# A graph layer's edge loop: six of every thirteen blocks of edges summed by matmuls instead of four of nine, with another beat of the accumulation stages

## The chip, the core and the metric

The kernel runs on one core of a Trainium2 chip. The core's engines work side by side: TensorE (PE in the profile, its weight loads PEld), VectorE (DVE), ScalarE (ACT) and GpSimd (POOL); SyncE (SP) issues most DMA transfers and POOL issues the scatters. Each engine runs its own instructions strictly in order, and semaphores tie them together. The metric is the time of one execution on the device in microseconds (us). Before the change the median of three runs is 2077.85 us (2071.54 to 2080.63).

## What is computed

One layer of a graph network over 6250 nodes with 128 features and 200,000 edges. An edge has a source (`src`), a destination (`dst`, sorted), 20 attributes and a weight. Node features go through a layer norm, a ReLU and a matrix; edge attributes go through a small network that gives a filter; each edge multiplies the gathered row of its `dst` by its filter, and the products are summed by `src`. Cut to what matters:

```python
idx_i, idx_j = src, dst
x = relu(layernorm(x0)) @ W_in
W_ij = shifted_softplus(f_ij @ W_f1 + b_f1) @ W_f2 + b_f2
W_ij = W_ij * f_ij_cutoff
x_ij = x[idx_j] * W_ij
out = segment_sum(x_ij, idx_i, num_segments=6250)
return x0 + shifted_softplus(out @ W_o1 + b_o1) @ W_o2 + b_o2
```

The sources are in random order, so the sum by source is the hard part, and the change is about how it is shared out.

## The kernel before

Edges are worked in quads of 512 (four chunks of 128 edges): 391 quads, and one iteration of a loop written out by hand for each, plus some at the end. In iteration i the kernel does the first matmul of quad i + 1 (`s1_pe`, tile z, L313), the activation of quad i on ACT (`s1_exp`, `s1_ln`, L318 and L323), and for quad i - 1 the gather by a one-hot matmul (`s2_pe_x`, xg, L497), the second matmul (`s2_pe_w`, W, L505), the scaling on ACT (`s2_copy`, xc, L510) and the product on DVE (`s2_m`, L520).

The products are then summed by source in one of three ways, fixed for each quad:

- **Plain quads.** A one-hot comparison on DVE and four fp32 matmuls (`s3_pe`, pp, L532) merge equal sources within a chunk, ACT copies the result (L540), and four indirect DMAs on POOL's queue add the rows to one of four accumulators in HBM (`scatter`, L582, index tile ji).
- **Listed quads.** The product goes straight into four scatters (index tile lji). Rows whose source occurs twice in a chunk go to a list area behind the accumulator instead. Sixteen quads share a window; its list (128 rows per accumulator) is prepared by small steps (`l_eq`, `l_count`, `l_scan`, `l_index`, `l_place`, ...), and twelve iterations after the window's last quad it is read back (`l_load`), summed (`l_sum`), copied by ACT into a tile os (`l_copy`, L475) and scattered once.
- **Grouped quads.** No scatter for the rows themselves. Ranks are worked out for eight grouped quads at a time (`rank_*`). DVE builds one-hots (`perm_oh`, pm, L662) and splits the product into three bf16 parts (`part_rem`, L676); TensorE permutes the 512 rows into 16 groups of 32 slots by source range, in four slices of 128 slots (`permute`, pq, L687, 16 matmuls), and ACT copies the slices out (`perm_out`, tile mst, L693). Rows that found no slot go to an overflow (`over_pe`, po, L702 to L704; `over_out`, mo, L710); two quads' overflow is summed (`over_row`, `over_eq`, `over_sum`), copied by ACT into a tile os (`over_copy`, L746) and scattered once (index tile oji).

Eight grouped quads make a round, and a round has four units, one for each slice s. A unit is 96 small bf16 matmuls (`unit_pe`, un, L781) into four PSUM banks; before it DVE builds eight one-hots (`unit_oh`, so, L766) in the two iterations ahead, and after it DVE adds the four banks to accT in SBUF (`unit_evac`, L792).

PSUM has eight banks: four with the tag A (z, xg, W) and four with the tag B, which permute, overflow, pp, units, lists, ranks, the preparation of nodes (`prep_*`, one group every nine iterations until iteration 216) and others share in the order of the program. A unit takes all four B banks. Tiles rotate through a fixed number of buffers: pm and pt have two, the scattered tiles s four, os two (shared by overflow and lists).

The order is written by hand. `at(i, point, fn, ...)` hangs a step into iteration i at a named point: "L" (loads), "D0" and "D1" (DVE, early), "A0" and "A1" (ACT, before the scaling), "DM" (before the product), "PE2" (TensorE, last in the iteration), "A2", "D2" and "S" (scatters). `clear(i, units)` moves a step out of iterations that hold a unit.

Which quads are grouped follows from `MP0` (the first) and `MPGAPS` (the steps between them, repeated); which iterations hold units from `UOFF`, offsets within one repeat of `MPGAPS` counted from `MP0`; the first that comes five iterations after a round's last quad starts its units. With `MP0 = 8`, `MPGAPS = (2, 2, 2, 3)` and `UOFF = (2, 6)`, quads 8, 10, 12, 14, 17, ... 383 are grouped (168 of them, 21 rounds), and units stand in iterations 28, 32, 37, 41, 46, ... 383, then 389, 391, 393, 395. Of the other 223 quads, 192 in the middle are listed (12 windows) and 31 plain (12 at the start, 19 at the end).

A grouped quad q is permuted two slices in iteration q + 3 and two in q + 4 ("PE2"), with the copies at "A0" of the iterations after. When q + 4 holds a unit (40 quads), all four slices, their copies and the overflow are put into iteration q + 3 instead, ahead of the unit.

After the loop the accumulators are read back, summed with accT, and go through the last two matrices.

Of the kernel before, what the change touches and what calls it, by code (L numbers as in the profile page):

```python
# [7 lines left out]
F32 = mybir.dt.float32  # L8
# [12 lines left out]
P = 128  # L21
# [3 lines left out]
CAP = 32  # L25
OVC = 64
SLOTS = GRP * CAP + OVC
MP0 = 8
MPGAPS = (2, 2, 2, 3)
MPEND = 0  # L30
RND = 8
EXTRA = 0
RKQ = 8
UOFF = (2, 6)
SW = 16
LEARLY = 8
LLATE = 16
# [17 lines left out]
def tile_gnn(ctx: ExitStack, tc: tile.TileContext, x, fB, cT, srcT, srcr, dstr, win_, wf1, wf2, bias, bo1c, wo1,  # L55
             wo2, consts, ident, cmap, out, n_edges):
    nc = tc.nc
# [20 lines left out]
    ZL = 3  # L78
# [4 lines left out]
    units = unit_its(mpq)  # L83
# [11 lines left out]
    LR = P * NW  # L95
# [13 lines left out]
    sp_ = edge.enter_context(tc.tile_pool(name="sp", bufs=4))  # L109
# [31 lines left out]
    zero = accT[:, :ACC_R // ZR]  # L141
# [27 lines left out]

    def zero_list(k, j):  # L170
        v = accs[k][ACC_R:].rearrange("(p t) f -> p (t f)", p=P)
        w = LR // ZL
        nc.sync.dma_start(v[:, j * w:(j + 1) * w], zero[:, :w])

    def xt_load(g):
        o, T = groups[g]
# [294 lines left out]
        mp["L", j]["sum"] = t  # L471

    def l_copy(j):
        s = sp_.tile([P, 132], F32, tag="os", name="os", bufs=2)
        nc.scalar.copy(s[:, :P + 1], mp["L", j].pop("sum")[:, :P + 1])  # L475
        mp["L", j]["os"] = s

# [264 lines left out]
        mp[q]["sum"] = t  # L742

    def over_copy(q):
        s = sp_.tile([P, 132], F32, tag="os", name="os", bufs=2)
        nc.scalar.copy(s[:, :P + 4], mp[q].pop("sum")[:, :P + 4])  # L746
        mp[q]["os"] = s

# [87 lines left out]
    with tc.manual_schedule():  # L836
# [112 lines left out]
        def at(i, point, fn, *a):  # L949
            hooks.setdefault((i, point), []).append((fn, a))  # L950
# [6 lines left out]
        if CE < EP // P:  # L957
            w = (CE + 4 * NS) // 2
# [128 lines left out]
        if spread:  # L1087
            k = clear(mid + 9, busy, 2)
# [3 lines left out]
            k = clear(NQ - 1, busy, 2)  # L1092
# [21 lines left out]
        for r in range(-(-len(mpq) // RKQ)):  # L1114
            i = mpq[RKQ * r]
            at(i - 5, "D2", rank_group, r)
            k = clear(i - 4, units)
            at(k, "PE2", rank_count, r)
            at(k + 1, "D0", rank_own, r)
            k = clear(k + 1, units)  # L1120
# [5 lines left out]
        for w in range((LE - LB) // SW):  # L1126
# [25 lines left out]
            k = clear(i + 1, units)  # L1152
            at(k - 1, "L", l_load, w)
            at(k, "PE2", l_sum, w)
            at(k + 1, "A0", l_copy, w)
            at(k + 1, "DM", l_ji, w)
            at(k + 1, "A2", over_int, ("L", w))
            at(k + 2, "S", over_scatter, ("L", w))
        if LE:
            for k in range(NACC):  # L1160
                for j in range(ZL):
                    at((0, 3, 6, 9)[k] + j + 1, "L", zero_list, k, j)
        for q in mpq:
            at(q + 1, "D2", perm_oh, q)
            at(q + 2, "D2", part_rem, q, 1)
            at(q + 2, "D2", part_rem, q, 2)
            at(q + 2, "A2", part_ext, q)
            if q + 4 in units:
                for s in range(4):
                    at(q + 3, "PE2", permute, q, s)  # L1170
                for s in range(4):
                    at(q + 3, "PE2", perm_out, q, s)
                at(q + 3, "PE2", over_pe, q)
                at(q + 3, "PE2", over_out, q)
            else:
                for s in range(4):
                    at(q + 3 + s // 2, "PE2", permute, q, s)
                    at(q + 4 + s // 2, "A0", perm_out, q, s)
                at(q + 4, "PE2", over_pe, q)
                at(q + 5, "A0", over_out, q)  # L1180
            if q == mpq[-1] and mpi[q] % 2 == 0:
                at(q + 4, "D2", over_none, q)
            if mpi[q] % 2 or q == mpq[-1]:
                at(q + 5, "DM", over_idx, q)
                at(q + 6, "A0", over_dg, q)
                k = clear(q + 6, units)
                at(k, "PE2", over_row, q)
                at(k + 1, "D0", over_eq, q)
                k = clear(q + 8, units)
                at(k, "PE2", over_sum, q)  # L1190
                at(k + 1, "A0", over_copy, q)
                at(k + 1, "DM", over_ji, q)
                at(k + 1, "A2", over_int, q)
                at(k + 2, "S", over_scatter, q)
# [85 lines left out]
    with tc.For_i(0, trips, 1) as ci:  # L1280
# [43 lines left out]
        a = wk.tile([P, P], F32, tag="a", name="fa")  # L1324
# [11 lines left out]
        s = wk.tile([P, P], F32, bufs=1, tag="dg", name="fs")  # L1336
# [112 lines left out]
def sorted_quads(nq):  # L1449
    qs, q = [], MP0  # L1450
    while q < nq - MPEND:
        qs.append(q)
        q += MPGAPS[(len(qs) - 1) % len(MPGAPS)]
    return qs if len(qs) % RND <= EXTRA else qs[:len(qs) // RND * RND]
# [7 lines left out]
def unit_slots(qs, r):  # L1462
    if r == len(qs) // RND - 1:
        return [qs[-1] + 6 + 2 * s for s in range(4)]
    per, end = sum(MPGAPS), qs[RND * r + RND - 1] + 5
    return [i for i in range(end, end + 4 * per) if (i - MP0) % per in UOFF][:4]

# [7 lines left out]
def unit_its(qs):  # L1475
    return {i for r in range(len(qs) // RND) for i in unit_slots(qs, r)}


def clear(i, busy, n=1):
    while any(i + k in busy for k in range(n)):  # L1480
        i += 1
    return i
# [113 lines left out]
```

## Time and profile before

| | |
|---|---|
| Median of three runs | 2077.85 us |
| The profiled execution | 2069.4 us |
| Its span on the core | 2067.6 us |
| Mean granted TensorE clock | 0.963 |
| First scatter issued at | 55.24 us |
| Last scatter issued at, and its duration | 2006.32 us, 1.54 us |
| Scatters (L582): listed, plain, os | 768, 123, 96 |

The profile is of one execution. Its page gives busy time by engine, the span in slices, the DMA queues, a chain of work that ended last and the costliest groups of instructions; the trace behind it can be asked for stretches of time, for waits and for single instructions. In a group's line stand the line, the engine, the operation, the tiles (written from read), the shapes and the count; then busy time in us and the mean duration of one in ns; then the idle time just before these instructions and what ended it. A matmul's duration in the profile reaches into the next one's, since they are pipelined: what one costs is read from the distance between starts. In a timeline line stand the start, the duration (from the first start to the last end of a run of like instructions) and, in brackets, the idle time before it.

### The profile page before, as it was taken

Reading aid. Unit: us, or ns where it says so; the run is one execution under the profiler, and the core shown is the slowest. Engines: PE = TensorE matmul, PEld = TensorE weight load, DVE = VectorE, ACT = ScalarE, POOL = GpSimd, SP = SyncE. Lnnn points to the kernel's source line nnn. Section 1 sums busy time; section 2 is a strip of 40 time slices with the busy share of each in tenths; the row PEclk is TensorE's granted clock in tenths of the full one; section 3 lists DMA queues with packets and bytes.
Section 4 is the critical chain, followed back from the end, with each engine's and each line's share of the span. In section 5 each row is a group of like instructions: output and inputs, shape, how many; then the busy total and the mean of one; then the engine's idle time right before and its main releaser. Section 6 shows DMA issues by size and latency. Waiting matters only on the chain. (4 is left out here: it accounts for less than half of the span.)

```text
span 2067.6 us, 57535 instructions
## 1 busy us (share of the span) xinstructions
PE 1854.7 (90%) x20381; PEld 1285.7 (62%) x20381; DVE 1657.1 (80%) x4448; ACT 1490.1 (72%) x4083; POOL 1631.5 (79%) x1040
## 2 busy tenths in 40 slices
PE   3489997999999999999999999999999999999956
PEld 2356664666666666666666666666666666677734
DVE  3578896898987888988988978979889787787735
ACT  3368775777776788777778777777778678888714
POOL 3578888888877788887878878888888888888774
PEclk9689998999999999999999999999999999999978
DMA  7887766767766776766667666676676676667648
GB/s 240 227 211 150 125 124 109 128 112 135 130 124 106 126 133 117 136 124 122 121 133 123 122 123 117 118 129 107 129 128 116 112 126 111 110 120 131 129 46 242
DMA packets 381187, 272.56 MB, mean 132 GB/s; under 512 B 97727, under 2 KB 341354, under 8 KB 380898
## 3 DMA queue, kind: packets, MB, share of 16 engines
q0 software_dynamic: 143728, 71.30, 34.9%
q1 hardware_dynamic: 236882, 197.50, 33.8%
q8 instruction: 161, 2.64, 0.5%
q14 instruction: 128, 1.05, 0.2%
q10 hardware_dynamic: 288, 0.07, 0.0%
HBM read 154.45 MB, written 114.24 MB: 130 GB/s over the span
## 5 line engine op out<-in xcount | busy, mean ns | idle before, releaser
L582 POOL DMA_INDIRECT acc<-s,lji x768 | 1237.3, 1611 | 266.9 <-issue 184.6
L687 PE MATMUL pq<-pt,pm 128*128 128x387 bf16 x2688 | 527.9, 339 | 27.0 <-DVE pt L676 10.7
L510 ACT ACTIVATE xc<-xg,cb 128x128 f32<-128x128 f32 x1564 | 446.4, 371 | 121.0 <-PE xg L497 113.8
L505 PE MATMUL W<-w,a 128*128 128x128 f32 x3128 | 464.1, 293 | 0.0
L505 PEld LDWEIGHTS W<-w,a 128*128 128x128 f32 x3128 | 388.7, 196 | 42.0 <-issue 2.6
L781 PE MATMUL un<-so,mst 32*128 32x392 bf16 x8064 | 378.3, 331 | 31.9 <-ACT os L746 19.3
L693 ACT CAST mst<-pq 128x387 bf16<-128x387 f32 x672 | 303.1, 481 | 132.6 <-PE pq L687 130.0
L687 PEld LDWEIGHTS <-pm 128*128 128x128 bf16 x2688 | 259.4, 99 | 211.4 <-issue 16.7
L781 PEld LDWEIGHTS <-mst 32*128 32x128 bf16 x8064 | 228.4, 94 | 175.0 <-issue 70.0
L323 ACT ACTIVATE a<-a,con 128x512 f32<-128x512 f32 x391 | 282.3, 722 | 12.7
L582 POOL DMA_INDIRECT acc<-s,ji x123 | 197.0, 1602 | 82.8 <-issue 25.9
L318 ACT ACTIVATE a<-z 128x512 f32<-128x512 f32 x391 | 237.4, 607 | 33.2 <-PE z L313 17.4
L676 DVE TENSOR_TENSOR pt<-pt 128x512 f32<-128x512 f32 x336 | 231.8, 690 | 5.8
L662 DVE TENSOR_SCALAR pm<-iot,pos 128x576 bf16<-128x576 f16 x672 | 221.4, 390 | 0.0
L520 DVE TENSOR_TENSOR s<-W,xc 128x512 f32<-128x512 f32 x192 | 131.9, 687 | 92.9 <-ACT xc L510 86.0
L792 DVE TENSOR_TENSOR accT<-un,accT 128x392 f32<-128x392 f32 x320 | 158.5, 558 | 58.4 <-PE un L781 58.2
L766 DVE TENSOR_SCALAR so<-iot,mst 128x392 bf16<-128x392 f16 x672 | 191.2, 344 | 5.5 <-PE un L781 5.4
L582 POOL DMA_INDIRECT acc<-os,oji x96 | 155.6, 1621 | 31.1 <-issue 16.2
L497 PE MATMUL xg<-wn,oh 63*128 63x128 bf16 x1564 | 157.2, 222 | 14.5 <-ACT xc L510 8.1
L313 PE MATMUL z<-ft,ws 123*128 123x512 bf16 x391 | 151.6, 388 | 16.1 <-POOL b2rep L927 9.3
L494 PE MATMUL W<-b2rep,onesb 64*128 64x512 bf16 x391 | 153.8, 393 | 0.0
L520 DVE TENSOR_TENSOR pt<-W,xc 128x512 f32<-128x512 f32 x168 | 115.2, 686 | 34.9 <-ACT xc L510 29.4
(209 smaller groups left out, 2431.1 us busy)
## 6 DMA issues: line engine op xcount, KB each, us to landing
rb<-reld SPq DMA_DIRECT2D x391, 64.0 KB
fsd<-f SPq DMA_DIRECT2D x49, 480.0 KB
ft<-fsd SPq DMA_DIRECT2D x195, 120.0 KB
sb<-src SPq DMA_DIRECT2D x169, 128.0 KB
fb<-in_fB_dram SPq DMA_DIRECT2D x49, 320.0 KB
ft<-fsd SPq DMA_DIRECT2D x195, 80.0 KB
wn<-tab SPq DMA_DIRECT2D x782, 15.8 KB
acc<-s,lji POOLq DMA_INDIRECT x768
```

Source lines behind the costliest of these rows:

```text
L318: nc.scalar.activation(a, st[q]["z"], AF.Exp)
L323: nc.scalar.activation(a, a, AF.Ln, bias=half, scale=0.5)
L505: nc.tensor.matmul(W[:, c, :], st[q]["a"][:, c * P:(c + 1) * P], w2, start=False, stop=(c == 3))
L510: nc.scalar.mul(xc[:, c, :], st[q]["xg"][:, c, :], late["c", q // CQ][:, 4 * (q % CQ) + c:4 * (q % CQ) + c + 1])
L520: nc.vector.tensor_tensor(m[:, :, :P], st[q]["W"], st[q]["xc"], op=ALU.mult)
L582: nc.gpsimd.indirect_dma_start(out=accs[k][:rows, :], out_offset=bass.IndirectOffsetOnAxis(ap=ji, axis=0), in_=s, in_offset=None, compute_ ...
L662: nc.vector.tensor_scalar(pm[:, c], iot[:, :SLOTS], rk[r]["pos"][:, 4 * j + c:4 * j + c + 1], None, op0=ALU.is_equal)
L676: nc.vector.tensor_tensor(pt[:, :, k * P:(k + 1) * P], a, high(a), op=ALU.subtract)
L687: nc.tensor.matmul(t[:, :PW], mp[q]["pm"][:, c, s * P:(s + 1) * P], high(mp[q]["pt"][:, c:c + 1, :PW])[:, 0], start=(c == 0), stop=(c == 3))
L693: nc.scalar.copy(mp[q]["ms", s][:, :PW], mp[q].pop(("q", s))[:, :PW])
L766: nc.vector.tensor_scalar(so, iotw[:, :GN], w[:, 3 * P // 2:3 * P // 2 + 1], None, op0=ALU.is_equal)
L781: nc.tensor.matmul(ts[g][:, :GN], mp[q]["ms", s][v, k * P:(k + 1) * P], mp[q]["oh"][v], start=(q == qs[0] and k == 0), stop=(q == qs[-1] a ...
```

## The change

`MP0` becomes 5, `MPGAPS` (2, 2, 2, 2, 2, 3) and `UOFF` (2, 7, 11). So six of 13 quads are grouped, from quad 5 on: 5, 7, 9, 11, 13, 15, 18, ... 384, 176 of them in 22 rounds. Three iterations of 13 hold a unit: 25, 29, 33, 38, 42, 46, 51, ... 384, then 390, 392, 394, 396. Of the other 215 quads 176 are listed (11 windows) and 39 plain (20 at the start, 19 at the end).

With these places, no grouped quad has a unit in iteration q + 4, and 56 have one in q + 3. The diff widens the rule for putting all four slices together: if q + 3 or q + 4 holds a unit, all four slices, copies and overflow go into the other one of the two.

The tile os gets four buffers for two. With 11 windows an accumulator's list area has 1408 rows, which three pieces do not divide evenly by columns, so the zeroing computes each piece's bounds. The rank steps for the first eight grouped quads move from iteration 3 to iteration 0, and with them everything that hangs on the first quads' places.

```diff
-MP0 = 8
-MPGAPS = (2, 2, 2, 3)
+MP0 = 5
+MPGAPS = (2, 2, 2, 2, 2, 3)
...
-UOFF = (2, 6)
+UOFF = (2, 7, 11)
...
     def zero_list(k, j):
         v = accs[k][ACC_R:].rearrange("(p t) f -> p (t f)", p=P)
-        w = LR // ZL
-        nc.sync.dma_start(v[:, j * w:(j + 1) * w], zero[:, :w])
+        a, b = j * LR // ZL, (j + 1) * LR // ZL
+        nc.sync.dma_start(v[:, a:b], zero[:, :b - a])
...
     def l_copy(j):
-        s = sp_.tile([P, 132], F32, tag="os", name="os", bufs=2)
+        s = sp_.tile([P, 132], F32, tag="os", name="os", bufs=4)
...
     def over_copy(q):
-        s = sp_.tile([P, 132], F32, tag="os", name="os", bufs=2)
+        s = sp_.tile([P, 132], F32, tag="os", name="os", bufs=4)
...
-            if q + 4 in units:
+            if q + 3 in units or q + 4 in units:
+                k = q + 3 if q + 4 in units else q + 4
                 for s in range(4):
-                    at(q + 3, "PE2", permute, q, s)
+                    at(k, "PE2", permute, q, s)
                 for s in range(4):
-                    at(q + 3, "PE2", perm_out, q, s)
-                at(q + 3, "PE2", over_pe, q)
-                at(q + 3, "PE2", over_out, q)
+                    at(k, "PE2", perm_out, q, s)
+                at(k, "PE2", over_pe, q)
+                at(k, "PE2", over_out, q)
             else:
```

## The prediction

> **What bounds the kernel now.** I read the page's totals first, then the costliest groups, the busy time by window, the waits, and last the timeline of single stretches. The totals put two engines near the span:
>
> ```profile
> PE 1854.7 (90%) x20381; PEld 1285.7 (62%) x20381; DVE 1657.1 (80%) x4448; ACT 1490.1 (72%) x4083; POOL 1631.5 (79%) x1040
> ```
>
> POOL's 79% hides more, as the groups show (busy and mean ns, then idle before and its cause):
>
> ```profile
> L582 POOL DMA_INDIRECT acc<-s,lji x768 | 1237.3, 1611 | 266.9 <-issue 184.6 <-DVE s L520 25.0 <-DMA acc<-s,lji 22.0
> L687 PE MATMUL pq<-pt,pm 128*128 128x387 bf16 x2688 | 527.9, 339 | 27.0 <-DVE pt L676 10.7 <-DVE rt L651 6.3 <-ACT mst L693 3.6
> L781 PE MATMUL un<-so,mst 32*128 32x392 bf16 x8064 | 378.3, 331 | 31.9 <-ACT os L746 19.3 <-DVE pr L627 6.8 <-ACT s L540 2.4
> ```
>
> A scatter takes 1.61 us, and the timeline of POOL has 0.30 us before nearly each one that waits for nothing: 1.91 us of queue. There are 768 + 123 + 96 = 987 (lists, plain quads, sums): 1885 us, between the first at 55 us and the end of the last at 2007.9. So POOL really waits only some 68 us in those 1953. By windows (busy of PE, PEld, DVE, ACT, POOL, then clock, DMA share, GB/s):
>
> ```profile
> 300.00:400.00 100.00, 84.58 (x942) 57.97 (x941) 74.90 (x201) 68.26 (x189) 81.63 (x51) 0.91 0.64 115
> 900.00:1000.00 100.00, 91.15 (x1012) 63.58 (x1011) 85.22 (x233) 74.93 (x210) 79.64 (x50) 0.98 0.70 125
> 1700.00:1800.00 100.00, 98.86 (x1119) 67.60 (x1119) 79.72 (x207) 79.79 (x219) 83.85 (x53) 1.00 0.65 109
> 1950.00:2000.00 50.00, 39.87 (x536) 29.16 (x534) 29.48 (x86) 15.83 (x50) 39.96 (x26) 0.93 0.47 56
> ```
>
> TensorE is 91 to 99% busy through the loop. POOL does 50 to 53 scatters per 100 us, and 52.4 would fill it: it has slack in the middle, none late. After 1950 POOL drains a backlog while the others fall idle. From a list quad's product (DVE L520) to its first scatter it is 20 us around 200 to 300 us, 0.3 to 8 in the middle and 8 to 10 between 1530 and 1780 (those rows compared). The four s buffers allow four list quads, some 35 us at this pace, so after 300 us POOL holds nobody through them. It does through the ring of two os tiles, once for long:
>
> ```profile
> ACT os L746 <- DMA acc<-os,oji: 18.2, 2, 13.8
> ```
> ```profile
> 361.25 0.27 ACT L746 COPY os<-osum 128x132 f32<-128x132 f32 x1 [13.77 <-DMA acc<-os,oji]
> ```
> ```profile
> 361.56 2.80 PE L781 MATMUL un<-so,mst 32*128 32x392 bf16 x32 [14.18 <-ACT os L746]
> ```
>
> Copies at 322.8 and 337.7 (the second a list's sum) had filled both; POOL reached the first one's scatter only at 357.9, behind lists, and the next copy and TensorE's unit stood until then. So: TensorE with ACT and DVE sets the pace in the middle, POOL early, in the tail, and nearly so from 1300 us.
>
> **What the parts cost.** TensorE's prices, from starts in the timeline:
>
> ```profile
> 1904.62 1.56 PE L687 MATMUL pq<-pt,pm 128*128 128x387 bf16 x8
> 1906.11 0.25 PE L702 MATMUL po<-pt,pm 128*64 128x131 bf16 x1
> ...
> 1906.94 0.39 PE L494 MATMUL W<-b2rep,onesb 64*128 64x512 bf16 x1
> ...
> 1908.26 0.38 PE L313 MATMUL z<-ft,ws 123*128 123x512 bf16 x1
> 1908.58 4.16 PE L781 MATMUL un<-so,mst 32*128 32x392 bf16 x96
> 1912.67 0.39 PE L494 MATMUL W<-b2rep,onesb 64*128 64x512 bf16 x1
> ```
>
> A grouped quad: two permute halves of 1.49, the overflow 0.83, four eighths of a unit of 4.09 (2.05), half of orow and osum (0.22 each: 0.22), ranks (27.2 us of rkp and rko over 168: 0.16). Sum 6.24. A listed quad: lcnt, lsum, orow, lid, lpre, 56.8 us over 192: 0.30. A plain quad: pp, 0.89 by its spacing. Every quad has 1.54 of W, xg and z besides.
>
> *More grouped quads.* 168 become 176, listed 192 become 176, plain 31 become 39. TensorE: +8 x 6.24 - 16 x 0.30 + 8 x 0.89 = +52 us. POOL: 768 to 704, 123 to 155, sums 96 to 99: 958 scatters, -29 x 1.91 = -55 us. DVE, by the same division of rows (L662, L676, L766, L792 and the small ones: 5.8 a grouped quad, 1.0 a listed, 1.0 a plain): +38. ACT (L693 1.80, others 1.1 a grouped quad; 0.06 a listed; 1.0 a plain): +30. Per iteration TensorE's bare work goes from 1.54 + (4 x 6.24 + 5 x 0.30)/9 = 4.48 to 1.54 + (6 x 6.24 + 7 x 0.30)/13 = 4.58 us, POOL's from 22.3 x 1.91/9 = 4.73 to 31.4 x 1.91/13 = 4.62. The bounds swap nearly. DVE's and ACT's added work lies beside TensorE's.
>
> *Places of the units.* Before, 40 quads do all their permuting right before a unit, so all four B banks wait for ACT's copies when the unit begins: those units take 4.38 instead of 4.09. After, 56 quads do it in the iteration after a unit, whose banks DVE empties in four adds of 0.56 (2.2 us), while W, xg and z take 1.54 and each permute 0.75, so the banks come in step. Gain 0.29 x 40 = 12 us; if the adds come late, each of 56 loses up to 1.5 us (the four permutes' banks all one drain late, less what 0.75 a permute covers), 84 at worst. I take a gain of 10, since the permutes that follow a unit before show no such wait (1.49 a half).
>
> *Four os buffers.* They take away 14.2 + 4.5 us of TensorE's waits (at 361 and 1634). The price if POOL then blocks elsewhere: 0 gain.
>
> *Earlier start.* First quad 5 for 8, first unit 25 for 28, ranks in iterations 0 and 3. TensorE is 41% busy from 20 to 60 us, with DMA ahead of it, which hides them; -8 to +8, I take 0. The list-zeroing transfers stay twelve on SP's queue, a twelfth smaller: nothing. One more iteration at the end (last unit 396 for 395) hides under POOL's drain.
>
> **The sum**, by starts of the z matmul (quads 20, 60, 220, 360, 390 at 156.6, 346.7, 1147.3, 1813.2, 1957.6: 4.75, 5.00, 4.76, 4.81 us an iteration):
> - quads 20 to 60: 4.75 is POOL's pace; TensorE gets one more unit and 0.10 x 40, POOL less: +4.
> - 60 to 220: +0.10 x 160 = 16, unit starts -5, os -14: -3.
> - 220 to 360: +14 by TensorE's price, -4 unit starts, -4.5 os: +5 if TensorE alone sets it; -15 if POOL does. Both nearly do: -5.
> - 360 to 390: +3. The drain: 19 plain quads close both kernels; the backlog of 8 to 10 us ahead of them goes: -9.
>
> Together -10. The profiled execution took 2069.4 us (span 2067.6 and 1.8 around it), so about 2059; the median is 8.4 higher, and 10 below it is **2068 us**.
>
> The Trainium skill (SBUF — State Buffer, "Who interferes with whom") says that a VectorE tensor_scalar in a two-port mode locks GpSimd out, descriptor writing included. The rows agree in kind: scatters take 1.54 at least and 1.61 on average, with 1344 such one-hots beside 987 scatters. By that rule 64 more one-hots would cost POOL 64 x (0.07 x 987/1344) = 3 us, an estimate that changes no case.
>
> **Rivals.**
> *A, POOL is the bound all along.* For: 68 us of waits in 1953, none from 1300 to 1800. Against: the lag of 0.3 to 8 us in the middle, where TensorE is at 92%. All 55 us would come: 2023.
> *B, TensorE becomes the bound and the regular beat is lost (slower).* Prep comes every nine iterations, as the old pattern does, so it always fell beside the same units; against 13 it drifts onto iterations with 16 permutes, where ACT has 4.7 us (L318, L323, four L510 by spacing, four L693, L710) and a prep's 1.1 to do against TensorE's 5.4 (1.54 + 2.98 + 0.83). Decides if TensorE stays at the 91 to 95% of the middle: 52/0.92 = +57, less the stall's 19 and the 9 of the drain: +29, 2107. For: po already waits for prep's h on ACT, 4.2 us in eight waits from 400 to 1300 us. Against: late windows at 97 to 99%.
> *C, the change's smoothing does nothing:* the os stall was backlog, which blocks the s tiles next, and units start no sooner. The forecast without 19 and 10: +19, 2097. Against: POOL's backlog shrinks with its work.
>
> **How the numbers follow.** Forecast 0.47, A 0.14, B 0.25, C 0.14. Half a per cent (10 us) is about what a measurement of this kernel tells from no change. The forecast's own range is 2050 to 2084, its middle just at that edge: faster 0.30, same 0.15, slower 0.02. A is faster. B is slower for 0.23, same for 0.02; C slower for 0.10, same for 0.04. Together 0.44, 0.21, 0.35. The range, 2030 to 2110, leaves out A's full gain (some 0.08, if A pays in full) and the part of B beyond its own price, late adds among it (some 0.11).
>
> **What would show it.** L582's counts 704, 155, 99 and cadence 1.91; no ACT os wait of over 1 us; units at 4.09 throughout; PE at 95% or more from 400 to 1300 us with POOL's waits grown there; z of quad 220 before 1147, of 360 before 1805; less than 45 us from z of 390 to the last scatter. Wrong if un or pq now waits for DVE's accT or ACT's mst in the iterations after units, or if PE stays at 92%.

## The result: 3.4% slower

The changed kernel takes 2149.31 us (median of four runs, 2147.18 to 2150.6) beside 2079.21 us of the kernel before: a ratio of 1.0344, 95% interval 1.0316 to 1.0371. Forecast was 2068 us; 2030 to 2110 was the range. The profiled execution's span is 2148.8 us, 81.2 over the one before.

The totals after:

```profile
PE 1929.5 (90%) x20993; PEld 1326.5 (62%) x20993; DVE 1681.2 (78%) x4547; ACT 1513.8 (70%) x4168; POOL 1593.0 (74%) x1011
```

The same groups as before (busy us, mean ns; then idle before and what ended it):

```profile
L582 POOL DMA_INDIRECT acc<-s,lji x704 | 1146.0, 1628 | 323.7 <-issue 163.2 <-DVE s L520 100.0 <-DMA acc<-s,lji 16.6
L687 PE MATMUL pq<-pt,pm 128*128 128x387 bf16 x2816 | 558.1, 342 | 11.2 <-ACT mst L693 6.1 <-DVE oeq L736 1.4 <-DVE pt L676 1.3
L781 PE MATMUL un<-so,mst 32*128 32x392 bf16 x8448 | 396.5, 329 | 33.8 <-ACT s L540 19.2 <-DVE rt L651 3.8 <-issue 1.9
```

And windows (columns as before):

```profile
300.00:400.00 100.00, 95.84 (x1121) 64.97 (x1119) 88.66 (x251) 77.08 (x213) 82.23 (x51) 1.00 0.69 127
900.00:1000.00 100.00, 95.89 (x1105) 65.26 (x1097) 86.39 (x246) 76.03 (x211) 79.92 (x49) 1.00 0.68 126
1700.00:1800.00 100.00, 97.71 (x1121) 66.18 (x1120) 84.50 (x233) 79.36 (x218) 84.14 (x53) 1.00 0.66 115
1900.00:2000.00 100.00, 91.35 (x982) 65.27 (x978) 71.68 (x185) 70.49 (x200) 62.22 (x39) 0.98 0.56 110
```

POOL was relieved: 29 scatters fewer, and its wait for a list quad's product (DVE s L520) grew from 25 to 100 us. Its queue starves; the others cannot supply it. TensorE's busy share stays at 90%, which says little: over the same stretch of 1600 us it was as busy as before, and did 0.9% fewer matmuls and 3% fewer quads (317 z matmuls for 327). A quad brings more matmuls in the changed kernel, so the two shares need not be alike. This is the stretch's line before (columns as in the windows above, the counts of instructions in brackets):

```profile
250.00:1850.00 1600.00, 1509.19 (x17115) 1036.86 (x17115) 1355.98 (x3687) 1217.76 (x3347) 1318.37 (x817) 0.98 0.68 122
```

and after:

```profile
250.00:1850.00 1600.00, 1508.43 (x16954) 1026.09 (x16952) 1325.48 (x3624) 1190.47 (x3284) 1250.81 (x770) 0.98 0.64 116
```

Every engine issued less in the same time, while all but POOL have more to do in all. By the starts of the z matmul, in us (two single executions, 81 us apart, where the medians are 70 apart):

| Quads | before | after | forecast for the step | measured |
|---|---|---|---|---|
| 0 to 20 | 132.1 | 135.5 | 0 | +3 |
| 20 to 60 | 190.1 | 205.5 | +4 | +15 |
| 60 to 220 | 800.6 | 828.4 | -3 | +28 |
| 220 to 360 | 665.9 | 685.8 | -5 | +20 |
| 360 to 390 | 144.4 | 163.7 | +3 | +19 |
| 390 to the end | 110.0 | 106.0 | -9 | -4 |

The last stretch of the loop is the plainest: 30 iterations, 19 plain quads to the end in both, and 19 us lost. Single iterations stand out there: 363, 367, 376 and 380 take 9.5, 8.8, 12.7 and 8.7 us, where none of the kernel before takes over 7.5 between 359 and 388. All four hold a unit. The timeline of iteration 363 after:

```profile
1893.74 1.05 PE L532 MATMUL pp<-m,eq 128*128 128x129 f32 x8
...
1894.68 1.14 ACT L510 ACTIVATE xc<-xg,cb 128x128 f32<-128x128 f32 x4
...
1894.73 0.34 PE L781 MATMUL un<-so,mst 32*128 32x392 bf16 x2
1895.70 0.61 ACT L318 ACTIVATE a<-z 128x512 f32<-128x512 f32 x1
...
1896.35 0.72 ACT L323 ACTIVATE a<-a,con 128x512 f32<-128x512 f32 x1
...
1896.97 0.63 ACT L540 COPY s<-pp 128x258 f32<-128x258 f32 x2
1897.38 1.92 PE L781 MATMUL un<-so,mst 32*128 32x392 bf16 x34 [2.31 <-ACT s L540]
```

Quad 361 is plain. Its merging matmuls (pp) fill two of the four B banks right before the unit, which wants all four; ACT empties them only in the next iteration, after xc and two activations. The unit starts, stops after two matmuls, and TensorE stands for 2.31 us. In the kernel before the beat excludes this: pp belongs to the quad two iterations back, units stand at offsets 2 and 6, and the quads at offsets 0 and 4 are grouped. Only two of its last four units, in iterations 389 and 391, meet a plain quad. After, units stand at 2, 7 and 11, and offsets 5 and 9 are not grouped; eight plain quads meet a unit. In all, TensorE's units waited 2.4 us for ACT's s before, and after (us, times, longest):

```profile
PE un L781 <- ACT s L540: 19.2, 7, 5.6
```

Iteration 376, the longest, has more in it:

```profile
1965.74 0.29 ACT L755 ACTIVATE oji<-ojd,con 128x1 int32<-128x1 f32 x1 [2.27 <-DMA acc<-os,oji]
...
1967.28 0.85 ACT L693 CAST mst<-pq 128x387 bf16<-128x387 f32 x2
...
1968.45 0.35 PE L781 MATMUL un<-so,mst 32*128 32x392 bf16 x2
...
1972.08 5.13 PE L781 MATMUL un<-so,mst 32*128 32x392 bf16 x81 [3.29 <-ACT s L540]
```

Before anything else ACT stands 2.27 us at the index tile oji, whose two buffers a late scatter holds; so its copies of pq, xc and pp all come late. And once TensorE has stood, its granted clock (the first figure behind the five busy times, 0.50) is half for the start of the unit:

```profile
1972.00:1974.00 2.00, 1.92 (x25) 1.07 (x28) 2.00 (x5) 1.47 (x5) 1.70 (x2) 0.50 0.40 45
```

A second place shows among the waits after (us, times, longest):

```profile
PE rko L612 <- DVE ov L632: 15.8, 15, 2.5
PE lsum L469 <- DMA lm<-acc: 8.4, 4, 4.0
```

A round's two rank matmuls are one iteration apart in all 22 rounds after; a unit's iteration lay between them in 19 of 21 before, in which VectorE made ov. The list's rows (lm) also arrive late more often: 3.0 us before.

### The profile page after: what moved, and what is told of

It reads as the page before. It is cut to its first block, busy times and chain, and to the rows that moved or that the text cites. A ratio compares the mean times of both kernels' runs of the same rounds, so it can differ in the third digit from the quotient of the medians.

```text
span 2148.8 us, 58959 instructions
## 1 busy us (share of the span) xinstructions
PE 1929.5 (90%) x20993; PEld 1326.5 (62%) x20993; DVE 1681.2 (78%) x4547; ACT 1513.8 (70%) x4168; POOL 1593.0 (74%) x1011
## 5 line engine op out<-in xcount | busy, mean ns | idle before, releaser
L582 POOL DMA_INDIRECT acc<-s,lji x704 | 1146.0, 1628 | 323.7 <-issue 163.2
L687 PE MATMUL pq<-pt,pm 128*128 128x387 bf16 x2816 | 558.1, 342 | 11.2 <-ACT mst L693 6.1
L693 ACT CAST mst<-pq 128x387 bf16<-128x387 f32 x704 | 321.0, 484 | 164.7 <-PE pq L687 133.5
L781 PE MATMUL un<-so,mst 32*128 32x392 bf16 x8448 | 396.5, 329 | 33.8 <-ACT s L540 19.2
L687 PEld LDWEIGHTS <-pm 128*128 128x128 bf16 x2816 | 277.4, 100 | 207.4 <-issue 28.9
L781 PEld LDWEIGHTS <-mst 32*128 32x128 bf16 x8448 | 239.8, 94 | 185.8 <-issue 78.0
L582 POOL DMA_INDIRECT acc<-s,ji x155 | 246.9, 1593 | 141.2 <-ACT ji L563 76.3
L323 ACT ACTIVATE a<-a,con 128x512 f32<-128x512 f32 x391 | 282.3, 722 | 12.7
L676 DVE TENSOR_TENSOR pt<-pt 128x512 f32<-128x512 f32 x352 | 243.2, 691 | 6.1
L662 DVE TENSOR_SCALAR pm<-iot,pos 128x576 bf16<-128x576 f16 x704 | 231.3, 390 | 0.0
L520 DVE TENSOR_TENSOR pt<-W,xc 128x512 f32<-128x512 f32 x176 | 121.0, 688 | 112.2 <-ACT xc L510 83.3
L520 DVE TENSOR_TENSOR s<-W,xc 128x512 f32<-128x512 f32 x176 | 120.5, 685 | 86.6 <-ACT xc L510 64.1
## 6 DMA issues: line engine op xcount, KB each, us to landing
wn<-tab SPq DMA_DIRECT2D x782, 15.8 KB
```

The source lines that it names most:

```text
L323: nc.scalar.activation(a, a, AF.Ln, bias=half, scale=0.5)
L520: nc.vector.tensor_tensor(m[:, :, :P], st[q]["W"], st[q]["xc"], op=ALU.mult)
L582: nc.gpsimd.indirect_dma_start(out=accs[k][:rows, :], out_offset=bass.IndirectOffsetOnAxis(ap=ji, axis=0), in_=s, in_offset=None, compute_ ...
L662: nc.vector.tensor_scalar(pm[:, c], iot[:, :SLOTS], rk[r]["pos"][:, 4 * j + c:4 * j + c + 1], None, op0=ALU.is_equal)
L676: nc.vector.tensor_tensor(pt[:, :, k * P:(k + 1) * P], a, high(a), op=ALU.subtract)
L687: nc.tensor.matmul(t[:, :PW], mp[q]["pm"][:, c, s * P:(s + 1) * P], high(mp[q]["pt"][:, c:c + 1, :PW])[:, 0], start=(c == 0), stop=(c == 3))
```

## The experiments

Ratios are to the kernel before, run beside each, with 95% intervals. A gain in us over the changed kernel, or over another run, is the difference of two ratios times 2079 us; the two intervals together leave it open by 6 to 10 us. The traces, one execution each, tell where the time went.

**Part of the change alone.** Four os buffers in the kernel before:

```diff
-        s = sp_.tile([P, 132], F32, tag="os", name="os", bufs=2)
+        s = sp_.tile([P, 132], F32, tag="os", name="os", bufs=4)
```

> The kernel before with four os buffers for two and nothing else. Theory 'ring' (the prediction's): the waits of 14.2 and 4.5 us go and come back in the time, 2060 us against 2079. Theory 'backlog': POOL was behind at that point, and the s tiles or the drain take the time over, 2075 to 2083.

0.9953 (0.9932 to 0.9975): some 10 us, between the two. The longest wait is still there, in other clothes; ACT's timeline of that run:

```profile
349.62 0.25 ACT L746 COPY os<-osum 128x132 f32<-128x132 f32 x1
364.71 0.29 ACT L755 ACTIVATE oji<-ojd,con 128x1 int32<-128x1 f32 x1 [13.80 <-DMA acc<-os,oji]
```

The copy passes, and ACT stands 13.80 us at the index oji, which belongs to the same scatter and also has two buffers. So that ring was opened too:

```diff
-        ji = sp_.tile([P, 1], I32, tag="oji", name="oji", bufs=2)
+        ji = sp_.tile([P, 1], I32, tag="oji", name="oji", bufs=4)
```

and ojd, three to four.

> The kernel before with four buffers each for os, for the integer index oji and for its float ojd (two, two and three before). With os alone the wait of 13.8 us did not go but moved to oji, whose ring of two is held by the same scatter. Theory 'ring': now it goes, another 10 to 15 us, a ratio of 0.986 to 0.992 against 0.9953. Theory 'backlog': it moves on to the s tiles, 0.994 to 0.997.

0.9906 (0.9881 to 0.9932): 2055.09 us beside 2073.57. The wait did not move on to the s tiles: ACT's and VectorE's waits for them are 16.2 us in that run's trace, 14.9 before. Of the kernels here that leave nothing out, this is the fastest.

**What the kernel before is bound by.** POOL's part of the change, with a scatter left out in each of 29 listed quads:

```diff
-            for c in range(nchunks(q)):
+            for c in range(nchunks(q) - int((plain[q] - LB) % 6 == 3 and plain[q] - LB < 174)):
```

> The kernel before with 29 of the 768 scatters of listed quads left out (one of four in every sixth quad, its rows missing from the sums): POOL's part of the change alone, 55 us of its queue. Theory 'POOL paces': 45 to 55 us, 2025 to 2035 against 2080. The prediction's reading (POOL paces only early and in the drain): 5 to 20 us, 2060 to 2075. Theory 'not POOL': under 5.

0.9977 (0.9958 to 0.9996): some 5 us of the 55.

TensorE's, with two thirds of the overflow's matmuls left out:

```diff
-            nc.tensor.matmul(o[:, :P + 3], w, pt[:, 2 * P:PW], start=(c == 0), stop=False)
-            nc.tensor.matmul(o[:, :P], w, pt[:, P:2 * P], start=False, stop=False)
-            nc.tensor.matmul(o[:, :P], w, pt[:, :P], start=False, stop=(c == 3))
+            nc.tensor.matmul(o[:, :P + 3], w, pt[:, 2 * P:PW], start=(c == 0), stop=(c == 3))
```

> The kernel before, leaving out two of the three parts of the overflow's products (8 of 12 matmuls of each grouped quad, L703 and L704, 0.48 us by their starts): 168 x 0.48 = 81 us less on TensorE, everything else as it was; the overflow rows are then sums of the last part alone. Theory 'TensorE paces' : nearly all of it comes, 65 to 85 us, 1995 to 2015 us against 2080. Theory 'POOL paces' (the prediction's case A): POOL's 987 scatters at 1.91 us still need 1885 us after the first 55, so 10 to 30 us at most, 2050 to 2070.

0.9919 (0.9892 to 0.9946): 17 us of the 81. And both edits at once:

> The kernel before with both taken away, the 81 us of TensorE's work (which alone gave 0.992) and the 29 scatters (which alone gave 0.998). Theory 'two bounds close together': each hid the other, and together they give clearly more than their sum, 0.970 to 0.982. Theory 'neither, waits among TensorE, ACT and DVE set the pace': the sum, 0.988 to 0.992.

0.9831 (0.9805 to 0.9857): 35 us, where the two alone add to 22. They hide each other in part, but 136 us of work taken from the two fullest engines bring only 35. What holds the rest these runs do not show. Waits among TensorE, ACT and VectorE are one candidate; TensorE's clock is another. With the overflow's matmuls left out, the mean granted clock of the five runs is 0.952 to 0.957, beside 0.961 to 0.966 of the kernel before, and in the traces the clock stands at a half for 176 us instead of 153. If TensorE had paced all of that, the lower clock would have eaten some 16 us of the 81 (an estimate: 0.008 of 2055 us). The same overflow edit in the changed kernel:

> The changed kernel with the same 8 of 12 matmuls left out: 176 x 0.48 = 85 us less on TensorE. Theory 'work': TensorE paces the changed kernel, 70 to 90 us come, 2060 to 2080 us against 2149. Theory 'places': waits between TensorE, ACT and DVE pace it, and take a good part of what the matmuls gave, 25 to 55 us, 2095 to 2125.

1.0162 (1.0125 to 1.0199): 38 us of 85 come back, twice the share of before. TensorE counts for more in the changed kernel, but not for all. Here too the clock fell, to 0.955 to 0.958 from 0.964 to 0.968.

**The places.** First the collision, by copying pp out at once in units' iterations:

```diff
-            full[i] = sum(fn in banked for fn, _ in hooks.get((i, "PE2"), [])) > 2
+            full[i] = sum(fn in banked for fn, _ in hooks.get((i, "PE2"), [])) > 2 or i in units
```

> The changed kernel, with a plain quad's merged rows copied out by ACT in the same iteration when that iteration holds a unit (before, units stood where the quad two iterations back was grouped; now two of three stand where it may be plain, so the unit waits for two PSUM banks that ACT empties only an iteration later). Theory 'collision': iterations 363, 367, 376 and 380 took 8.7 to 11.1 us where the same places among listed quads take 5.9 to 6.6, and 25 and 29 are alike: about 4 us each, so 15 to 25 us come back, 2124 to 2134 us against the changed kernel's 2149. Theory 'work': the added matmuls alone, 2149, within 5.

1.0271 (1.0242 to 1.0301): 15 us. In the trace only some 8 us of it lie at these places (quads 20 to 60 and 360 to 390); the rest lies where the edit changes nothing. Iterations 363 and 367 fell from 9.5 and 8.8 to 8.3 and 7.1 us, so this shortens the wait and does not end it: the copies still come after xc. Iteration 376 did not fall at all (12.7 to 13.6). To take the collision away whole, in the changed kernel those quads skip pp:

```diff
     def s3_pe(q):
-        if not plainq(q):
+        if not plainq(q) or q + 2 in units:
             return
...
-        nc.scalar.copy(st[q]["s"][:, 2 * h:2 * h + 2, :129], st[q]["p"][h][:, :, :129])
+        src_ = st[q]["m"][:, 2 * h:2 * h + 2, :129] if q + 2 in units else st[q]["p"][h][:, :, :129]
+        nc.scalar.copy(st[q]["s"][:, 2 * h:2 * h + 2, :129], src_)
...
-        nc.scalar.activation(ji, st[q]["jf"], AF.Identity, bias=trash)
+        nc.scalar.activation(ji, st[q]["jf"], AF.Identity, bias=trash, scale=0.0 if q + 2 in units else 1.0)
```

ACT still copies, from the tile m, and the scatters go to spare rows.

> The changed kernel, where a plain quad whose merging matmuls would share an iteration with a unit skips them: ACT copies its product directly and its four scatters go to the spare rows behind the nodes, so its rows are missing from the sums. Eight quads (23, 27, 361, 365, 374, 378, 388, 390). The earlier repair took 15 us, but the unit still waits there for ACT's copies (8.6, 8.2, 8.3, 7.1 us an iteration for the 5.7 of others). Theory 'collision': all of it, 22 to 30 us, a ratio of 1.020 to 1.024 against 1.034. Theory 'the matmuls alone': 8 x 0.89 = 7 us, 1.031.

1.0217 (1.0192 to 1.0241): 26 us, give or take 8. The trace puts 15 of them at the eight quads (quads 20 to 60 5.9, 360 to the end 8.8), and 6 between quads 60 and 360, where the edit changes nothing. So the eight places are worth some 15 us, of which the matmuls left out are 8 x 0.89 = 7. That the collision is real is shown: the units' waits for ACT's s are gone, and iterations 25, 29, 363, 367 and 380 fall from 8.7 to 11.2 us to 5.7 to 6.6. Iteration 376 stays at 11.8 us; the collision is not what makes it long.

Next the banks held by the overflow's row and sum in iterations with 16 permutes:

```diff
-                k = clear(q + 6, units)
+                k = clear(q + 6, units | comps)
...
-                k = clear(q + 8, units)
+                k = clear(max(q + 8, k + 1), units | comps)
```

> The changed kernel, with the row and the sum of the overflow kept out of the iterations that do all 16 permutes (they hold a bank of tag B, so that four permuted slices go through two or three banks in step with ACT's copies). Theory 'banks': those iterations took 5.7 to 6.8 us where the fastest take 5.48; half a microsecond to one at some 50 places, 2110 to 2130 us. Theory 'work': 2149, within 5.

1.0441 (1.0407 to 1.0475): 20 us worse. As a repair this falls, but the trace bears the idea out: the 50 iterations with 16 permutes between 34 and 358 take 5.66 us on average for 6.33, 33 us in all, of which the moved rows' own matmuls, one row in each, are about a third (50 x 0.22). The other iterations of that stretch, where the steps were moved to, take 50 us more. So these places did cost time before the edit; this edit pays more elsewhere. Why the iterations after lose so much was not run.

The ranks, one iteration apart more:

```diff
-            k = clear(k + 1, units)
+            k = clear(k + 2, units)
             at(k, "PE2", rank_over, r)
```

> The changed kernel with the ranks' second matmul one iteration later, so that VectorE has an iteration between (in the kernel before a unit always stood between the two; in the changed one they share an iteration, and TensorE waited for VectorE's ov 14 times, 15 us). Theory 'places': 10 to 16 us come, a ratio of 1.027 to 1.030 against 1.034. Theory 'other waits take it over': 1.032 to 1.036.

1.0313 (1.0287 to 1.0339): 6 us. The wait for ov, 15.8 us, is gone from the list of waits. How much of it is in the time is not settled: the intervals of 1.0313 and 1.0344 overlap, and the two traces differ by 15 us from quad 20 to 360, where nearly all the ranks stand.

The preparation on the beat of 13. It needs one more tile in memory (leqt), for which os goes back to three buffers:

```diff
-PREP_GAP = 9
+PREP_GAP = 13
...
-        eq = wk.tile([P, P], F32, tag="rm", name="leq", bufs=1)
+        eq = wk.tile([P, P], F32, tag="leqt", name="leq", bufs=1)
...
-            i = mid + 8 * (t // 4) if spread else 0
+            i = mid + 10 * (t // 4) if spread else 0
```

> The changed kernel with one preparation of nodes every 13 iterations instead of nine, so that it falls on the same place of the 13-iteration beat each time (it then goes on to iteration 320 instead of 216; three os buffers, a tile of its own for the list's comparison, and the bias added to the node features a little later). Theory 'beat lost' (the prediction's case B): iterations 60 to 210 lose 0.3 us each over their fastest more than in the kernel before, up to 45 us come back, 2105 to 2130. Theory 'work': the same preparations elsewhere, 2149, within 10.

1.0288 (1.0259 to 1.0317): 12 us. Quads 60 to 220 took 807.8 us for 828.4, but 220 to 360, where preparation now goes on, 698.4 for 685.8. The first stretch also has fewer preparations now, 12 or 13 for some 18, so its 21 us are not the beat's alone: 13 of them come back with the preparations that moved, and the beat is worth the 8 that are left.

The edits for pp and for preparation together:

> The changed kernel with both repairs, plain quads' rows copied out in the iterations of units and the preparation every 13 iterations, which gave ratios of 1.027 and 1.029 to the kernel before, alone, where the changed kernel has 1.034. If they are two independent costs they add: 1.021 to 1.023, 2122 to 2127 us. If they are the same waits met twice: 1.027, 2135.

1.0261 (1.0220 to 1.0301): 17 us, less than the 27 of the two, and its interval holds both expectations. Iteration 376 is still at 13.7 us. All repairs, which adds to these the ranks, an earlier load of the list's rows, and deeper rings for oji (two to four) and ojd (three to four):

```diff
-            k = clear(k + 1, units)
+            k = clear(k + 2, units)
...
-            at(k - 1, "L", l_load, w)
+            at(k - 2, "L", l_load, w)
```

> The changed kernel with all repairs: rows of plain quads copied out in units' iterations, preparation every 13 iterations, ranks apart, lists read back an iteration earlier, four buffers for oji and ojd (three for os). The first two gave 1.026. Theory 'places': ranks 13 us, lists 8 and less, 1.014 to 1.020. If more matmul work is what is left, it stays above 1.010.

1.0152 (1.0124 to 1.0181): 40 us of the 70 come back. By the traces it is 11 of the 15 lost in quads 20 to 60, 18 of 28 in 60 to 220, 12 of 19 in 360 to 390, and nothing in 220 to 360. Not all of it is places: this is the first run of the changed kernel with four oji buffers, and with them ACT's wait for the scatter is gone and iteration 376 falls from 13.7 to 7.7 us. So some 6 us look like the ring's; that edit was not run alone. Then the skipping of pp on top:

> The same leaving out, on top of all repairs (1.0152 before). Theory 'collision': the copies' rest, 8 to 15 us, 1.008 to 1.011. Theory 'work': 7 us at most, 1.012 to 1.015.

1.0122 (1.0097 to 1.0147): another 6 us, of the order of the matmuls left out; the intervals of the two runs overlap. Iteration 376 is at 5.7 us now, where it stayed at 11.8 with the skipping alone. And last, about the added TensorE work, one of the overflow's three matmuls left out on top of that, 42 us in all:

```diff
-            nc.tensor.matmul(o[:, :P], w, pt[:, P:2 * P], start=False, stop=False)
```

> The same, leaving out also one of the three parts of the overflow's products (L703: 4 of 12 matmuls of each grouped quad, 176 x 0.24 = 42 us), about as much TensorE work as the change adds (52 less the 7 left out before). Theory 'work' for what is left: near half of it comes, as in the changed kernel, 15 to 25 us against the run beside it, and the kernel stands at 0.998 to 1.003. Theory 'more places': under 10 us, 1.004 to 1.010.

1.0027 (1.0013 to 1.0041): 20 us of the 42. With places and rings mended and the work taken away, the changed kernel is within 6 us of the kernel before. That one still has its short rings: with four buffers it stands at 0.9906, and beside that some 25 us stay unaccounted for.

## Why the prediction was wrong, step by step

- **The places of the units: the step that failed.** It was put as a gain of 10, after a look at the banks between units and permutes alone. The gain is there for some: units at about 4.1 us rose from 35 to 42, those at 4.2 to 4.5 fell from 26 to 14. But longer ones rose from 23 to at least 31, and what else stands in the units' iterations was not looked at. A beat of nine held pp, ranks and preparation at one fixed place against the units and permutes; 13 iterations broke that. Measured in place of the gain: the units' waits for ACT's s went from 2.4 to 19.2 us, TensorE's for ov from 0.5 to 15.8, and repairs and the leaving out take the ratio from 1.0344 to 1.0122, some 46 us of the 70 (7 of them matmuls, some 6 the oji ring). In the sum these are losses in the stretches 20 to 60, 60 to 220 and 360 to 390, where +4, -3 and +3 were put and +15, +28 and +19 came. The 20 us lost from 220 to 360 the repairs together did not give back.
- **Case B had the sign and half the size.** It named preparation's drift (12 us by its repair) and TensorE as the bound, at +29. It missed the collision of plain quads with units (some 15 us with its matmuls), ranks and lists.
- **More grouped quads: the 52 us of TensorE's work** were counted right, and the forecast charged 0.10 us an iteration, full price. The runs charge near half: 20 of 42 in the mended kernel, 38 of 85 in the changed one. So of the 70 us work is some 20 to 25, as an estimate: those runs take other matmuls away than the change adds, and the clock falls with them. Where it counts the traces show: from quad 220 to 360 the overflow's matmuls left out gave 20.6 us in the changed kernel (685.8 to 665.2) and nothing in the kernel before (665.9 to 666.7). There the forecast let POOL's relief outweigh TensorE's added work, -5, and TensorE's work came through.
- **POOL's relief** was priced nearer than in case A, and still too high: the forecast had 9 us for the drain and took 10 off the stretch 220 to 360, case A had 55, and 29 scatters fewer in the kernel before gave 5. The price of 0.07 us that the prediction puts on a scatter beside VectorE's one-hots does not come out of its rows: in the trace before, 383 scatters that overlap one for over 0.1 us take 1.616 us on average, the other 604 take 1.608.
- **Four os buffers:** 18.7 us were forecast, and that is what the ring is worth (0.9906 is 18 us beside its runs), but two tiles hold it. With os alone the kernel before gains 10. In the changed kernel, whose oji kept two buffers, that ring closes once, in iteration 376: ACT's wait is only 2.3 us, but by the runs with four oji buffers the iteration lost some 6 by it. Whether the four os buffers would be missed was not run.
- **The drain** gave 4 of the 9: from z of quad 390 to the last scatter's end 46.4 us for 50.3.
- **What would show it wrong** was put as waits for accT or mst after units. Those stayed small; the waits came from ACT's s and VectorE's ov, at places not on the list. Two named marks failed plainly: z of quad 220 came at 1193 and not before 1147, and TensorE's share from 400 to 1300 us went from 94.4 to 93.4% and not to 95.

Open are single shares: the repairs of lists, of rings and of ranks together with the rest were run only as a sum, and they do not add.

## What to carry to other kernels

A hand-written beat keeps steps apart by offsets that nobody wrote down; before changing its period, list for every heavy step what shares its iteration and its buffers, in the special stretches at both ends too. When a wait for a buffer is removed, look for every tile that the same late consumer holds: here the next ring of the same length took the wait over unchanged (13.77 us, then 13.80). Moving work from one full engine to another gained nothing here, where both were near the limit; take work out of each alone first to see what it is worth. And when a repair fails as a whole, look in its trace at the places it was meant for: here they did get faster, and others paid.

## What the runs showed of the hardware

The busy time of TensorE does not tell matmuls done: 1509 and 1508 us in 1600, with 17115 and 16954 matmuls, at the same granted clock of 0.98. The busy time of its weight loads did follow, from 1036.9 to 1026.1 us. A matmul's end is modelled in the profile, so short waits can count as busy: an engine at 94% could lose 81 us of its work, and the kernel only 17.

A stall of TensorE cost more here than its own length. After the stall that the prediction shows at 361 us, 32 matmuls of the unit take 2.80 us, 0.09 each, where 96 take 4.16 elsewhere, 0.04 each; the granted clock stands at 0.5 there for 17.1 us, from 349.5 on. Taking matmuls away lowered the clock as well: the four kernels without part of the overflow have means of 0.955 to 0.958 over their runs, the kernel before 0.962 to 0.963 beside them.
